# A graph layer's edge loop: where the softmax's exponentials, maxima and values stand in its steps

## The chip, the cores and the metric

The kernel runs on one core of one Trainium2 chip. The metric is the device time of one execution in microseconds. Before the change it is 4211.2 us, the median of three runs (4210.71 to 4215.71).

## The reference

12500 nodes with 128 features, 400000 edges in the order of their targets. Rows of node features are normalized and clipped, projected twice, gathered to the edges, weighted, and summed back to the targets with a softmax per target and head. Cut to what matters (`h` is the normalized input):

```python
message = (h @ w_src + b_src)[edge_src] + (h @ w_dst)[edge_dst]
rad_w = silu(silu(edge_attr_32 @ w1 + b1) @ w2 + b2) @ w3 + b3
message = (message * edge_weight1 * rad_w) @ w_sep + b_sep      # 8 heads of 16 + 16
alpha = smooth_leaky_relu(message[:, :, :16]); value = message[:, :, 16:]
score = einsum('ehk,ahk->eh', alpha, alpha_dot)
att = segment_softmax(score, edge_dst)                          # maximum, exp, sum per target
out = segment_sum(value * att, edge_dst) @ w_proj + b_proj
return x + out
```

`smooth_leaky_relu` contains a sigmoid, which the kernel computes through SiLU.

## The kernel before

A first stage normalizes the nodes and writes both projected tables (`t_src`, `t_dst`) to memory. The main loop, `step(k)` in `windows()`, then goes over the edges in NP = 391 pairs of sections; a section is SEC = 512 edges, a pair 1024. Its order is written out by hand: the functions are called in a fixed order in each step, and each engine runs its own instructions in that order. A step works on several pairs at once:

- `gather(k+2, f)` (L867): POOL issues 8 indirect transfers, one per 128 edges, into buffers of which there are three for each half `f`. `sources(k, f)` (L934) transposes the rows on PE into the banks `pm0` and `pm1`.
- The MLP on the edge attributes: `e_T(k+3)` (L877, L879), `mlp1(k+2)` (L886, two SiLUs at L890), `mlp2(k+1)` (L901, SiLU at L904), `mlp3(k)` (L918), `radial(k)` (L926).
- `split_md` (L852 to L859) cuts the targets' rows into three bf16 parts, on ACT and DVE in turn; `message(k)` (L941, L948) adds them and multiplies.
- `alphas(k-1, f)` (L954, SiLU at L956) and `alphas_sum` (L961); in odd steps `scores(k-2)` (L970, and `Sp` by an Identity on ACT, L987), whose result goes to memory, and once in MP = 8 steps comes back as `S_all` of a macro of 16 sections (L993).
- The softmax of macro m - 1 while macro m runs. With r = k modulo 8: `softmax_up` (L1003, L1008) at the end of r = 2, a scan for the running maximum; `softmax_down` (L1013), the scan back, and `softmax_exp` (L1018 subtraction, L1020 Exp, two stores of maxima at L1029) at the end of r = 3; `softmax_T` (L1035 transposes, L1038 copy) in two halves in r = 4.
- `weights(c)`, `values(c, f)`, `one_hot(c)` and `sums(c-1)` (L1045, L1065, L1067, L1051, L1078, L1082) with c = k - LAG, LAG = 13: values times weights, summed into windows of 64 targets by a product with a one-hot. The last loop steps, after k = NP, hold only this work (the tail). `store_win` and `store` (L1086, L1090) write the windows through SP. Stores to `agg` from step 384 on are declared free of the scatters (`2 * c + 1 >= (NC - 1) * (P // 2)`, NC = 13).

PSUM has few banks: the bank `misc` (`half` is its first half) serves the second half of `mlp1`, the window sums and the softmax's transposes in turn; the bank `m1` serves the first half of `mlp1`, the scores, the transposes of `e_T` and the spread of marks for the scans; `pa` and `V` have one buffer each.

Targets that cross a section's end are put together in blocks of 128 section ends: `block_load` and `block_rows`, `block_maxima`, `block_factors` (with two exponentials, L1158, L1159), `block_columns`, `block_totals`, `block_out`, run in the loop at fixed steps of each 32 (`stages`, from k = LATE + 32 j, LATE = 32 + LAG + 2) and for the last two blocks in the tail (`jobs`). In the tail the finished blocks are read back (`comb<-obs_d`) and scattered to `agg` by POOL (L1197). A last stage divides, projects and adds the input.

ACT computes SiLU and Exp with different function tables; a table is loaded (ACT_TABLE_LOAD) where the function changes.

Of the kernel before, what the change touches and what calls it, by code (L numbers as in the profile page):

```python
# [49 lines left out]
PR = 2 * SEC  # L50
MP = 8
MQ = 2 * MP
LAG = 13


@with_exitstack
def gnn_kernel(ctx: ExitStack, tc: tile.TileContext, a: dict, out: bass.AP):
# [694 lines left out]
    def windows():  # L752
# [7 lines left out]
        with tc.tile_pool(name="ps", bufs=1, space=PSUM) as pp, \  # L760
# [120 lines left out]
            def mlp1(k):  # L881

                p1 = [pp.tile([P, 2 * T], F32, name="m1"), half[:, 0:2 * T]]
                for q in range(2):
                    s = slice(q * 2 * RAD, (q + 1) * 2 * RAD)
                    nc.tensor.matmul(p1[q], w1b[s, :], eTs[k][s, :], start=True, stop=True)  # L886
                h1s[k] = sp.tile([P, SEC], F32, name="h1")
                h1v = h1s[k].rearrange("x (f p q) -> x q f p", f=2, q=2)
                for q in (1, 0):
                    nc.scalar.activation(h1v[:, q], p1[q].rearrange("x (f p) -> x f p", f=2),  # L890
                                         AF.Silu, bias=b12[:, 0:1], scale=1.0)
# [45 lines left out]
            def message(k):  # L937
                for j in range(3):
                    for f in range(2):
                        s, n = slice(f * W, (f + 1) * W), tiles(k, f) * T  # L940
                        nc.tensor.matmul(pms[k, f][:, 0:n], m3[k][s, j, :], ohT[k][s, 0:n],  # L941
                                         start=False, stop=(j == 2), skip_group_check=True)
                rad = rads.pop(k)
                mTs[k] = sp.tile([C, PR], F32, name="mT", bufs=LAG + 1)
                for f in range(2):
                    n = tiles(k, f) * T
                    s = slice(f * SEC, f * SEC + n)
                    nc.vector.scalar_tensor_tensor(mTs[k][:, s], pms.pop((k, f))[:, 0:n], b_n, rad[:, s],  # L948
                                                   op0=ALU.add, op1=ALU.mult)
# [64 lines left out]
                                             op0=ALU.add, op1=ALU.max)  # L1014

            def softmax_exp(m):
                M = Ms[m]
                nc.vector.tensor_sub(M[:, 0, :], S_all[m], M[:, 1, :])  # L1018
                Ps[m] = sp.tile([P, SEC], F32, name="Pr", bufs=1)
                nc.scalar.activation(Ps[m], M[:, 0, :], AF.Exp)  # L1020
                with nc.allow_non_contiguous_dma(reason="the maxima at the sections' ends"):
                    n = min(MQ, NS - m * MQ)
                    whole = MQ if n == MQ else n - 1
                    for e, q0, q1, o in ((0, 0, n, 0), (1, 0, whole, SEC - 1),
                                         (1, whole, n, E - 1 - (NS - 1) * SEC)):
                        if q1 > q0:
                            at = max_d[0:1, (m * MQ + q0) * 2 + e:(m * MQ + q0) * 2 + e + 1]
                            at = bass.AP(at.tensor, at.offset, [[2, q1 - q0], [2 * NS, H], [1, 1]])
                            nc.sync.dma_start(out=at, in_=M[q0 * H:q1 * H, 1, o:o + 1])  # L1029

            def softmax_T(m, i):
                pt = half[:T, :].rearrange("p (t q) -> p t q", t=TS // 2)
                t0 = i * (TS // 2)
                for t in range(TS // 2):
                    nc.tensor.transpose(pt[:, t, :], Ps[m][:, (t0 + t) * T:(t0 + t + 1) * T], ident)  # L1035
                if i == 0:
                    Pem[m] = sp.tile([T, TS, MQ, H], F32, name="Pem")
                nc.scalar.copy(Pem[m][:, t0:t0 + TS // 2].rearrange("p t q h -> p t (q h)"), pt)  # L1038
# [98 lines left out]

            def block_maxima(g):
                w, node = width(g), nodes.pop(g)
                differ[g] = sp.tile([P, P + 1], BF16, name="differ", bufs=1)  # L1140
                nc.vector.tensor_tensor(differ[g][:, 0:w], node[:, 1:w + 1], node[:, 0:w], op=ALU.not_equal)
                cuts[g] = sp.tile([P, P], BF16, name="cuts", bufs=1)
                nc.vector.tensor_scalar(cuts[g][:, 0:w], differ[g][:, 0:w], RESTART, None, op0=ALU.mult)
                ups[g] = sp.tile([P, P + 1], F32, name="up", bufs=2)
                if g:
                    nc.vector.tensor_copy(ups[g][:, 0:1], ups[g - 1][:, P:P + 1])
                else:
                    nc.vector.memset(ups[g][:, 0:1], 0.0)
                nc.vector.tensor_tensor_scan(ups[g][:, 1:1 + w], cuts[g][:, 0:w], mxs[g][:, 0:w],
                                             ups[g][:, 0:1] if g else RESTART, op0=ALU.add, op1=ALU.max)  # L1150

            def block_factors(g):
                w, up, mx = width(g), ups[g], mxs[g][:, 0:width(g)]
                de = des[g] = sp.tile([P, P], F32, name="de", bufs=2)[:, 0:w]
                nc.vector.tensor_add(de, up[:, 0:w], cuts.pop(g)[:, 0:w])
                nc.vector.tensor_sub(de, de, up[:, 1:1 + w])
                nc.vector.tensor_sub(mx, mx, up[:, 1:1 + w])
                nc.scalar.activation(de, de, AF.Exp)  # L1158
                nc.scalar.activation(mx, mx, AF.Exp)  # L1159
                nc.vector.tensor_mul(mx[:, 1:w:2], mx[:, 1:w:2], differ.pop(g)[:, 1:w:2])  # L1160

            def block_columns(g):
                w, rr = width(g), rrs.pop(g)
                rx = sp.tile([P, C], F32, name="rx", bufs=1)
                nc.scalar.copy(rx[:w].rearrange("p (h k) -> p h k", h=H),
                               rr[:w, C:ROW].unsqueeze(2).to_broadcast([w, H, C // H]))
                pt = small()
                nc.tensor.transpose(pt[:, 0, 0:w], rr[:w, 0:C], ident[:w, :w])
                nc.tensor.transpose(pt[:, 1, 0:w], rx[:w, :], ident[:w, :w])
                mx = mxs.pop(g)  # L1170
                tots[g] = [sp.tile([P, P], F32, name=n, bufs=2) for n in ("rn", "rd")]
                for k, r in enumerate(tots[g]):
                    nc.vector.tensor_mul(r[:, 0:w].rearrange("p (s i) -> p i s", i=2),
                                         pt[:, k, 0:w].rearrange("p (i s) -> p i s", i=2),
                                         mx[:, 0:w].rearrange("p (s i) -> p i s", i=2))
# [30 lines left out]
            def combined(g):  # L1206
# [1 line left out]
                return comb[g]  # L1208

            stages = {0: lambda g: (block_load(g), block_rows(g)), 2: block_maxima, 4: block_factors,  # L1210
                      5: block_columns, 6: block_totals, 8: block_out}
            assert LAST_M * MP == (NC - 1) * SB and NP - LAST_M * MP < MP and LATE + (NC - 3) * SB + 8 < NP


            def has(k):
                return 0 <= k < NP
# [4 lines left out]
            def step(k):  # L1221
# [54 lines left out]
                    split_md(k + 1, 2)  # L1276
                if has(k + 2):
                    mlp1(k + 2)
                if has(k):
                    mlp3(k)  # L1280
                if has(k + 1):
# [13 lines left out]
                if k == NP:  # L1295
                    alphas_sum(k - 1, 1, *alphas(k - 1, 1))
                    scores(k)
                if has(c):
                    values(c, 1)
                if has(k - MP) and r == 4:  # L1300
                    softmax_T(m - 1, 0)
                if has(k - 1) and k < NP:
                    sl = alphas(k - 1, 1)
                if has(k):
# [10 lines left out]
                    alphas_sum(k - 1, 1, *sl)  # L1315
                if has(k):
                    message(k)
                if has(k + 1):
                    mlp2(k + 1)
                if has(k - MP) and r == 4:  # L1320
                    softmax_T(m - 1, 1)
                if has(k - MP):
                    if r == 2:
                        softmax_up(m - 1)
                    elif r == 3:
                        softmax_down(m - 1)
                        softmax_exp(m - 1)
                j, o = divmod(k - LATE, SB)
                if 0 <= j < NC - 2 and o in stages:
                    stages[o](j)  # L1330

# [10 lines left out]
            def out_rows(g):  # L1342
# [4 lines left out]
                0: lambda: block_load(last - 1),  # L1347
                1: lambda: block_maxima(last - 1),
                2: lambda: block_factors(last - 1),
                5: lambda: block_load(last),  # L1350
                6: lambda: block_maxima(last),
                7: lambda: (block_factors(last), block_rows(last - 1)),
                8: lambda: block_columns(last - 1),
                9: lambda: block_totals(last - 1),
                10: lambda: out_rows(last - 1),
            }
            assert SB * (NC - 1) + LAG + 1 == NP + 7
            for k in range(NP, NP + LAG + 1):
                step(k)
                j = k - NP  # L1360
# [162 lines left out]
```

## Time and profile before

| what | value |
|---|---|
| median of three runs | 4211.2 us |
| the profiled execution | 4210.06 us, span of its instructions 4208.2 us |
| mean granted clock of TensorE | 0.978 |
| busy: PE, DVE, ACT, POOL | 93%, 74%, 45%, 72% of the span |
| gathers (L867) | 3125, 951 ns each |
| table loads on ACT | 49 to Exp at L1020, 48 back to SiLU at L956, 1283 ns each |
| PE's weight load at L1078 waiting for ACT's SiLU at L890 | 392.7 us in 371 waits |
| PE at L1078 waiting for the same | 108.2 us in 48 waits |

A row of a timeline has start, duration, engine, line, operation, output and inputs, count, and in brackets the idle time of the engine before it with what ended that. An instruction that only issues a transfer is shown with a q behind the engine's name. Loads of weights (PEld) overlap products (PE) and may wait long without PE standing.

### The profile page before, as it was taken

The numbers are of one execution on the slowest core, as the hardware profiler recorded it, in microseconds if no ns is written. First come the engines' busy times: TensorE is split into PE (matmuls) and PEld (weight loads), VectorE is DVE, ScalarE is ACT, GpSimd is POOL, SyncE is SP. The second block draws the span as 40 slices with busy tenths as digits, with TensorE's granted clock in tenths as the row PEclk, the third lists the DMA queues.
The fourth block names the chain that finished last, engine by engine and source line by source line (L and its number), as shares of the span: only waits on it lengthen the run. The fifth ranks groups of instructions, "written<-read, shape, count | busy, mean of one in ns | idle before, by whom it ended". The sixth has DMA issues, their size and how long they took to land. (4 is left out here: it accounts for less than half of the span.)

```text
span 4208.2 us, 87881 instructions
## 1 busy us (share of the span) xinstructions
PE 3917.1 (93%) x29351; PEld 2391.0 (57%) x29351; DVE 3103.4 (74%) x6187; ACT 1901.6 (45%) x4549; POOL 3009.4 (72%) x3195
## 2 busy tenths in 40 slices
PE   6789999999999999999999999999999999999975
PEld 6345555555555555555555555555555555555555
DVE  5567777777777777777777777777777777777754
ACT  5344444444444444444444444444444444444421
POOL 4767777777777777777777777777777777777710
PEclk8999999999999999999999999999999999999988
DMA  7766777777776776777777776776777676776624
GB/s 249 233 173 187 191 187 187 197 192 180 199 192 179 196 195 174 195 195 188 188 192 194 181 193 180 178 188 182 178 191 184 183 184 183 188 180 180 184 84 160
DMA packets 593334, 783.08 MB, mean 186 GB/s; under 512 B 125554, under 2 KB 392303, under 8 KB 592741
## 3 DMA queue, kind: packets, MB, share of 16 engines
q1 hardware_dynamic: 384786, 514.16, 40.9%
q0 software_dynamic: 100416, 205.44, 23.6%
q10 hardware_dynamic: 107666, 57.76, 4.6%
q8 instruction: 234, 3.83, 0.4%
q14 instruction: 232, 1.89, 0.2%
HBM read 637.83 MB, written 139.30 MB: 185 GB/s over the span
## 5 line engine op out<-in xcount | busy, mean ns | idle before, releaser
L867 POOL DMA_INDIRECT gs<-t_src,idx x3125 | 2971.5, 951 | 978.8 <-issue 801.7
L956 ACT ACTIVATE sl<-pa,c_b_a 128x512 f32<-128x512 f32 x782 | 536.9, 687 | 1021.1 <-PE pa L954 1009.5
L961 DVE SCALAR_TENSOR_TENSOR al<-pa,sl 128x512 f32<-128x512 f32 x782 | 539.8, 690 | 596.6 <-ACT sl L956 577.1
L1065 PEld LDWEIGHTS V<-c_w_v,mT 128*128 128x128 f32 x6048 | 746.7, 194 | 292.1 <-DVE ob L1082 119.1
L1065 PE MATMUL V<-c_w_v,mT 128*128 128x128 f32 x6048 | 879.3, 289 | 0.0
L954 PE MATMUL pa<-mT,c_w_a 128*128 128x512 f32 x1564 | 816.1, 604 | 4.0 <-DVE mT L948 3.0
L1067 DVE TENSOR_TENSOR pvx<-V,Pem 128x512 f32<-128x512 f32 x756 | 517.7, 685 | 243.8 <-PE V L1065 232.0
L934 PEld LDWEIGHTS pm<-ident,gs 128*128 128x128 f32 x3125 | 393.0, 142 | 422.1 <-issue 316.9
L1078 PEld LDWEIGHTS misc<-pvx,oh 128*64 128x64 f32 x6250 | 353.0, 137 | 407.8 <-ACT h L890 392.7
L926 DVE SCALAR_TENSOR_TENSOR rad<-p,c_fc_b,w_b 128x512 f32<-128x512 f32 x782 | 550.0, 745 | 40.1 <-PE p L918 3.5
L1078 PE MATMUL misc<-pvx,oh 128*64 128x136 f32 x6250 | 454.2, 287 | 115.4 <-ACT h L890 108.2
L948 DVE SCALAR_TENSOR_TENSOR mT<-pm,c_b_src,rad 128x512 f32<-128x512 f32 x782 | 550.6, 746 | 2.2 <-PE pm L941 2.2
L904 ACT ACTIVATE h<-p,b 128x512 f32<-128x512 f32 x391 | 287.6, 735 | 422.7 <-PE p L901 367.9
L934 PE MATMUL pm<-ident,gs 128*128 128x128 f32 x3125 | 471.0, 273 | 0.0
L918 PE MATMUL p<-h,w3b 64*128 64x512 f32 x1564 | 405.2, 595 | 14.4 <-ACT h L904 14.4
L941 PE MATMUL pm<-ohT,m 64*128 64x512 bf16 x2346 | 321.8, 380 | 0.0
L987 ACT ACTIVATE Sp<-m,b_s 128x512 f32<-128x512 f32 x192 | 131.9, 687 | 393.9 <-PE m L970 389.8
L886 PE MATMUL m<-eT,w1b 64*128 64x256 f32 x782 | 274.3, 431 | 17.9 <-DVE M L1008 16.7
L886 PE MATMUL misc<-eT,w1b 64*128 64x256 f32 x782 | 274.3, 431 | 0.0
L1051 DVE TENSOR_TENSOR oh<-lane,misc 128x504 f32<-128x504 f32 x391 | 261.3, 668 | 0.0
L901 PE MATMUL p<-h,w2b 64*64 64x256 f32 x3128 | 259.7, 402 | 1.0 <-DVE rad L926 1.0
L954 PEld LDWEIGHTS pa<-mT,c_w_a 128*128 128x128 f32 x1564 | 242.2, 196 | 20.0 <-DVE mT L948 7.1
(172 smaller groups left out, 3651.0 us busy)
## 6 DMA issues: line engine op xcount, KB each, us to landing
w_b<-in_edge_weight SPq DMA_DIRECT2D x390, 512.0 KB
d_b<-in_dst SPq DMA_DIRECT2D x390, 256.0 KB
gs<-t_src,idx POOLq DMA_INDIRECT x3125
e_t<-in_edge_attr ACTq DMA_DIRECT2D x390, 128.0 KB
sc_d<-Sp SPq DMA_DIRECT2D x192, 256.0 KB
win<-ob SPq DMA_DIRECT2D x391, 68.0 KB
agg<-ob SPq DMA_DIRECT2D x782, 33.5 KB
md<-t_dst SPq DMA_DIRECT2D x782, 32.0 KB
```

What stands on the lines that cost most here:

```text
L867: nc.gpsimd.indirect_dma_start(out=gs[:, t, :], out_offset=None, in_=t_src[:, :], in_offset=bass.IndirectOffsetOnAxis(ap=idx[:, t0 + t:t0 ...
L886: nc.tensor.matmul(p1[q], w1b[s, :], eTs[k][s, :], start=True, stop=True)
L918: nc.tensor.matmul(p3s[k][:, f, 0:SEC], w3b[s, :], h2s[k][s, :], start=True, stop=True)
L926: nc.vector.scalar_tensor_tensor(rad[:, s], p3[:, f, 0:n], b3, w_g[k][:, s], op0=ALU.add, op1=ALU.mult)
L934: nc.tensor.matmul(pms[k, f][:, t * T:(t + 1) * T], gs[:, t, :], ident, start=(t == 0), stop=False, is_transpose=True, skip_group_check=True)
L948: nc.vector.scalar_tensor_tensor(mTs[k][:, s], pms.pop((k, f))[:, 0:n], b_n, rad[:, s], op0=ALU.add, op1=ALU.mult)
L954: nc.tensor.matmul(pa[:, 0:n], w_a, mTs[k][:, f * SEC:f * SEC + n], start=True, stop=True)
L956: nc.scalar.activation(sl[:, 0:n], pa[:, 0:n], AF.Silu, bias=b_a, scale=1.0)
L961: nc.vector.scalar_tensor_tensor(al, pa, 0.25, sl, op0=ALU.mult, op1=ALU.add)
L1065: nc.tensor.matmul(V[:, t, :], mTs[c][:, o:o + T], w_v, start=True, stop=True)
L1067: nc.vector.tensor_mul(pvx[c][:, f, 0:n, 0:C].rearrange("p t (h k) -> p t h k", h=H), V[:, 0:n, :].rearrange("p t (h k) -> p t h k", h=H), ...
L1078: nc.tensor.matmul(acc[f * W:(f + 1) * W, :], ohs[c][:, f * TS + t, :], pvx[c][:, f, t, :], start=(t == 0), stop=(t == n - 1), skip_group_ ...
```

## The change

The exponential of the softmax leaves the end of step r = 3 and is issued in the middle of that step, after `mlp1` and before `mlp3`; the two exponentials of a block come right behind it, out of `block_factors`. So that its operand is there, both scans and the subtraction move to r = 2: the scan up before the second half of the values, the scan down and the subtraction (with the stores of the maxima) at the step's end. Both halves of the transposes move from r = 4 to r = 3, one after `message`, one at the step's end. The values then follow 12 steps behind (LAG = 12, one buffer of `mT` less). The blocks' stages start a step earlier, and from `block_columns` on stand where they stood; a multiplication moves from `block_factors` to `block_columns`, for which `differ` gets a second buffer. In the tail all jobs stand a step earlier, and there is one step less.

```diff
-LAG = 13
+LAG = 12
...
             def softmax_exp(m):
+                Ps[m] = sp.tile([P, SEC], F32, name="Pr", bufs=1)
+                nc.scalar.activation(Ps[m], Ms[m][:, 0, :], AF.Exp)
+
+            def softmax_sub(m):
                 M = Ms[m]
                 nc.vector.tensor_sub(M[:, 0, :], S_all[m], M[:, 1, :])
-                Ps[m] = sp.tile([P, SEC], F32, name="Pr", bufs=1)
-                nc.scalar.activation(Ps[m], M[:, 0, :], AF.Exp)
...
                 nc.vector.tensor_sub(mx, mx, up[:, 1:1 + w])
-                nc.scalar.activation(de, de, AF.Exp)
+
+            def block_exp(g):
+                nc.scalar.activation(des[g], des[g], AF.Exp)
+                mx = mxs[g][:, 0:width(g)]
                 nc.scalar.activation(mx, mx, AF.Exp)
-                nc.vector.tensor_mul(mx[:, 1:w:2], mx[:, 1:w:2], differ.pop(g)[:, 1:w:2])
...
-                      5: block_columns, 6: block_totals, 8: block_out}
+                      6: block_columns, 7: block_totals, 9: block_out}
...
                 if has(k + 2):
                     mlp1(k + 2)
+                j, o = divmod(k - LATE, SB)
+                if has(k - MP) and r == 3:
+                    softmax_exp(m - 1)
+                    if 0 <= j < NC - 2 and o == 5:
+                        block_exp(j)
                 if has(k):
                     mlp3(k)
...
+                if has(k - MP) and r == 2:
+                    softmax_up(m - 1)
                 if has(c):
                     values(c, 1)
-                if has(k - MP) and r == 4:
-                    softmax_T(m - 1, 0)
...
                 if has(k):
                     message(k)
+                if has(k - MP) and r == 3:
+                    softmax_T(m - 1, 0)
                 if has(k + 1):
                     mlp2(k + 1)
-                if has(k - MP) and r == 4:
-                    softmax_T(m - 1, 1)
                 if has(k - MP):
                     if r == 2:
-                        softmax_up(m - 1)
+                        softmax_down(m - 1)
+                        softmax_sub(m - 1)
                     elif r == 3:
-                        softmax_down(m - 1)
-                        softmax_exp(m - 1)
-                j, o = divmod(k - LATE, SB)
+                        softmax_T(m - 1, 1)
...
-                5: lambda: block_load(last),
-                6: lambda: block_maxima(last),
-                7: lambda: (block_factors(last), block_rows(last - 1)),
-                8: lambda: block_columns(last - 1),
-                9: lambda: block_totals(last - 1),
-                10: lambda: out_rows(last - 1),
+                3: lambda: block_exp(last - 1),
+                4: lambda: block_load(last),
+                5: lambda: block_maxima(last),
+                6: lambda: (block_factors(last), block_exp(last), block_rows(last - 1)),
+                7: lambda: block_columns(last - 1),
+                8: lambda: block_totals(last - 1),
+                9: lambda: out_rows(last - 1),
```

More of the change, by code (lines that the diff above doesn't have):

```diff
@@ L1139, in block_maxima @@
                 w, node = width(g), nodes.pop(g)
-                differ[g] = sp.tile([P, P + 1], BF16, name="differ", bufs=1)
+                differ[g] = sp.tile([P, P + 1], BF16, name="differ", bufs=2)
                 nc.vector.tensor_tensor(differ[g][:, 0:w], node[:, 1:w + 1], node[:, 0:w], op=ALU.not_equal)
@@ L1170, in block_columns @@
                 mx = mxs.pop(g)
+                nc.vector.tensor_mul(mx[:, 1:w:2], mx[:, 1:w:2], differ.pop(g)[:, 1:w:2])
                 tots[g] = [sp.tile([P, P], F32, name=n, bufs=2) for n in ("rn", "rd")]
@@ L1210, in windows @@
             stages = {0: lambda g: (block_load(g), block_rows(g)), 2: block_maxima, 4: block_factors,
-                      5: block_columns, 6: block_totals, 8: block_out}
-            assert LAST_M * MP == (NC - 1) * SB and NP - LAST_M * MP < MP and LATE + (NC - 3) * SB + 8 < NP
+                      6: block_columns, 7: block_totals, 9: block_out}
+            assert LAST_M * MP == (NC - 1) * SB and NP - LAST_M * MP < MP and LATE + (NC - 3) * SB + 9 < NP and (LATE + 5) % MP == 3
             def has(k):
@@ L1349, in windows @@
                 2: lambda: block_factors(last - 1),
-                5: lambda: block_load(last),
-                6: lambda: block_maxima(last),
-                7: lambda: (block_factors(last), block_rows(last - 1)),
-                8: lambda: block_columns(last - 1),
-                9: lambda: block_totals(last - 1),
-                10: lambda: out_rows(last - 1),
+                3: lambda: block_exp(last - 1),
[5 more added lines that the diff above has]
+                9: lambda: out_rows(last - 1),
             }
-            assert SB * (NC - 1) + LAG + 1 == NP + 7
+            assert SB * (NC - 1) + LAG + 1 == NP + 6
             for k in range(NP, NP + LAG + 1):
```

## The prediction

> **What bounds the kernel now.** I read the page first, then the gather's line in windows, then POOL's timeline against PE's. The page's line of engines, and one group of it:
>
> ```profile
> PE 3917.1 (93%) x29351; PEld 2391.0 (57%) x29351; DVE 3103.4 (74%) x6187; ACT 1901.6 (45%) x4549; POOL 3009.4 (72%) x3195
> ...
> L867 POOL DMA_INDIRECT gs<-t_src,idx x3125 | 2971.5, 951 | 978.8 <-issue 801.7
> ```
>
> PE looks like the bound, and POOL like an engine with a quarter of its time free. It isn't free: 801.7 of its 978.8 idle us are "issue", time in which it waited for nothing that the profile shows. POOL's timeline near the start of the loop and at its end, then two windows with the gather's line alone (length, busy us and count, clock, DMA share, GB/s):
>
> ```profile
> 240.73 0.94 POOL L867 DMA_INDIRECT gs<-t_src,idx  x1 [0.83 <-PE pm L934]
> ...
> 4008.24 0.95 POOL L867 DMA_INDIRECT gs<-t_src,idx  x1 [0.30 <-issue]
> 4009.50 0.94 POOL L867 DMA_INDIRECT gs<-t_src,idx  x1 [0.30 <-PE V L1065]
> ```
> ```profile
> 240.50:4010.50 3770.00, 2852.06 (x3001) 0.99 0.71 187
> 587.10:1339.60 752.50, 569.59 (x600) 1.00 0.73 191
> ```
>
> A gather takes 0.94 to 0.95 us, and 0.30 us pass before the next. The window from 587.10 begins and ends with a gather's start: 600 in 752.5 us, 1.254 us each. From the gather at 240.73 to the last are 3000 spacings in 3768.8 us, 1.256 each. So POOL runs at nearly its own best rate all through the loop. A period of 8 steps needs 64 gathers, 64 x 1.254 = 80.3 us, however fast the others are.
>
> PE over one such period: windows cut at the start of the MLP's third product (one per step); the first is a plain even step, then the steps with r = 2 and r = 4 (r is the step modulo 8), then the whole period. Columns: length; PE, PEld, DVE, ACT, POOL busy.
>
> ```profile
> 1962.11:1971.01 8.90, 8.90 (x70) 5.60 (x68) 7.14 (x15) 3.89 (x11) 6.74 (x8) 1.00 0.85 240
> 1980.91:1990.13 9.22, 9.22 (x71) 5.69 (x69) 8.10 (x16) 3.84 (x11) 6.78 (x9) 1.00 0.74 196
> 2000.42:2012.66 12.24, 9.58 (x74) 6.02 (x72) 7.50 (x17) 7.10 (x19) 9.23 (x10) 1.00 0.72 136
> 1962.11:2041.37 79.26, 76.60 (x586) 46.09 (x584) 60.79 (x120) 37.36 (x90) 60.04 (x64) 1.00 0.75 197
> ```
>
> PE is busy from end to end but for one step: at r = 4 it stands 12.24 - 9.58 = 2.66 us, and that is all that it stands in the period (79.26 - 76.60). The period takes 79.3 us, just under POOL's 80.3; one with a block's work is above it. The two engines run level. The last full group of gathers is issued by 4008.24 + 0.95 = 4009.19, and PE takes it up here:
>
> ```profile
> 4031.20 0.60 PE L934 MATMUL pm<-ident,gs 128*128 128x128 f32 x4
> ```
>
> 22.0 us later. That lead is what PE can gain on POOL, and nearly all of it.
>
> **Part 1, the exponential leaves the end of the step.** The chain from r = 3 into 4, ACT's timeline, then PE's:
>
> ```profile
> 1998.01 1.28 ACT L1020 ACT_TABLE_LOAD   x1
> 1999.92 0.63 ACT L1020 ACTIVATE Pr<-M 128x512 f32<-128x512 f32 x1 [0.63 <-DVE M L1018]
> 2000.46 0.28 ACT L852 CAST m<-md 128x128 bf16<-128x128 f32 x1
> ...
> 2000.99 1.28 ACT L956 ACT_TABLE_LOAD   x1
> 2002.29 0.69 ACT L956 ACTIVATE sl<-pa,c_b_a 128x512 f32<-128x512 f32 x1
> ```
> ```profile
> 2003.61 0.34 PE L1078 MATMUL misc<-pvx,oh 128*64 128x136 f32 x2 [2.17 <-ACT h L890]
> ```
>
> Load, a wait of 0.63 us for the subtraction, Exp, and the load back push the next step's SiLUs back, and the window sums, whose bank they read, stand 2.17 us. The whole stall of the step is the 2.66 us above, and I take it to go. Changed, two loads and Exp, 1.28 + 0.63 + 1.28 = 3.2 us, lie between the first layer's SiLUs and the second alpha's SiLU of r = 3. ACT's idle gaps there now:
>
> ```profile
> 1993.30 0.69 ACT L987 ACTIVATE Sp<-m,b_s 128x512 f32<-128x512 f32 x1 [2.06 <-PE m L970]
> 1995.28 0.69 ACT L956 ACTIVATE sl<-pa,c_b_a 128x512 f32<-128x512 f32 x1 [1.29 <-PE pa L954]
> ```
>
> 2.06 + 1.29 = 3.35: it fits. A load is not held by its operand's wait (it ended at 1999.29, and Exp waited on), and the cast right behind Exp shows that a copy needs no load; Sp, an Identity, I take to be of that kind. Queued behind Exp are Sp, the second SiLU, the copy of eT with the issue of the next e_t load, the copy of Pem and the second layer's SiLU: some tenths late each. PE waits for Sp before the transposes of e_t, which share its bank. Taken 0; bounds 0 and 1.0 us a period, the upper one for the periods, one in four, in which a block's two exponentials come behind it.
>
> The Trainium skill, ScalarE: Activation LUTs, section What ACT_TABLE_LOAD costs, gives about 1283 ns for a load, as in the trace, and a drain of about 1380 ns beside it, which no row here shows: the SiLU starts 0.02 us after its load. By the page's 2.66 us a switch, an estimate, the move would be 2.6 us too long for its gaps and cost up to that.
>
> **Part 2, the maxima a step sooner.** Both scans and the subtraction now stand in r = 2 on DVE. Its timeline there, and the two operations that r = 3 has now:
>
> ```profile
> 1984.18 0.68 DVE L1067 TENSOR_TENSOR pvx<-V,Pem 128x512 f32<-128x512 f32 x1
> 1984.78 0.28 DVE L859 TENSOR_TENSOR m<-mr,m 128x128 bf16<-128x128 f32 x1
> 1985.78 0.69 DVE L961 SCALAR_TENSOR_TENSOR al<-pa,sl 128x512 f32<-128x512 f32 x1 [0.72 <-ACT sl L956]
> 1986.40 1.41 DVE L948 SCALAR_TENSOR_TENSOR mT<-pm,c_b_src,rad 128x512 f32<-128x512 f32 x2
> 1987.73 1.21 DVE L1008 TENSOR_TENSOR_SCAN M<-m,S 128x512 f32<-128x512 f32 x1
> ```
> ```profile
> 1997.95 1.21 DVE L1013 TENSOR_TENSOR_SCAN M<-m,M 128x512 f32<-128x512 f32 x1
> 1999.20 0.69 DVE L1018 TENSOR_TENSOR M<-S,M 128x512 f32<-128x512 f32 x1
> ```
>
> DVE is busy 7.14 of a plain even step's 8.90 us; 1.21 + 1.21 + 0.69 = 3.11 more make 10.25, in a step of 9.54 (two spreads of marks on PE at 0.32, from 9.22 - 8.90). DVE runs over by 0.7. Behind the late subtraction stand the product with V, the rest of md, its cast on ACT, the SiLUs behind that, and PE's window sums of r = 3. I count 0.5 us of PE there (a tenth or two of slack); bounds 0 and 1.9, the two operations that come new. The transposes go to r = 3 at their old cost. The stores of the maxima on SP wait for the same scan a step earlier; the stores and the loads behind them wait as they did. POOL's gathers are moved past nothing.
>
> PE's period is then 79.26 - 2.66 + 0.5 = 77.1 us against POOL's 80.3. PE uses up the lead in some ten periods, and from there on waits for gathers.
>
> **Part 3, the start.** The scan waited once for the scores' way through memory, and then POOL for PE:
>
> ```profile
> 222.70 1.22 DVE L1008 TENSOR_TENSOR_SCAN M<-m,S 128x512 f32<-128x512 f32 x1 [16.37 <-DMA S<-sc_d]
> ```
> ```profile
> 229.87 0.94 POOL L867 DMA_INDIRECT gs<-t_src,idx  x1 [9.15 <-PE m L877]
> ```
>
> The landing stays where it is (SP's queue ahead of it is the same), but the scan now stands ahead of half a step of DVE's work: 0.28, 0.69, 1.41, then the scan down and the subtraction, 1.21 + 0.69, before the next step goes on. POOL's wait grows by these 4.3 us (bounds 0 and 8).
>
> **Part 4, values 12 steps behind.** A step's products move from the tail into the loop, where POOL hides them, and the tail has a step less. Its steps are spaced so (SP, then POOL):
>
> ```profile
> 4080.70 1.81 SPq L1090 DMA_DIRECT2D agg<-ob  x2
> 4082.62 0.36 SPq L1364 DMA_DIRECT2D comb<-obs_d  x1
> ...
> 4087.37 1.83 SPq L1090 DMA_DIRECT2D agg<-ob  x2
> ```
> ```profile
> 4085.17 0.97 POOL L1197 DMA_INDIRECT agg<-comb,ids  x1 [5.69 <-DMA comb<-obs_d]
> ```
>
> A store to agg of a step below 384 waits for the scatter before it. The tail's first such step is 380 before and 381 after, so this chain has three links, not four: -6.7 us (bounds -3 and -10).
>
> **The sum,** against the profiled execution's 4210.06 us. The lead of 22.0 us shrinks to the time a gather takes to land. I take 2.5 us for it, an estimate from the transfer above (issued at 4082.62, awaited until 4085.17): -19.5. POOL's stream at 1.254 all through: 3000 x 1.2542 - 3768.8 = -6.2. Start +4.3, tail -6.7. Together -28.1: 4182.0. The median, 4211.2, is 1.1 above the profiled time: 4183. About 0.2%, 8 us, is what a measurement of this kernel can tell from no change.
>
> **Rivals.**
> (a) POOL can go faster, its 0.30 us being slack that PE's pace asks for. Then 2.66 - 0.5 us come in each of 48 periods: 4211.2 - 104 + 4.3 - 6.7, about 4105. For it speaks PE's 93%. Against it, the spacing of 1.254 holds in windows where POOL waits for no one. Chance 0.06. Perfetto Trace Analysis in the Trainium skill, section Identifying the Most-Contended Engine, measures GpSimd by occupancy; by that rule POOL at 72% bounds nothing, and this rival would be the forecast.
> (b) The stall only moves. DVE's overfull r = 2 and ACT's tight r = 3 cost the 2.7 us again; start and tail alone are left, 4211.2 + 4.3 - 6.7, so 4200 to 4212 with their bounds. For it: the upper bounds of parts 1 and 2 add to 2.9. Against: PE's waits there begin only where gaps of 3.35 are overfilled. Chance 0.17.
> (c) Slower: the first scan, in the middle of the step, comes before its scores have landed. Their load is issued here, and the scan would take the place of pvx at 1984.18, 6.5 us later, where it had 10.05:
>
> ```profile
> 1977.68 0.56 SPq L993 DMA_DIRECT2D S<-sc_d  x1
> ```
>
> The scan's row at 1987.73 shows no wait, so landing takes at most 10.05; DVE, and PE behind it, would stand up to 3.5 us in each period. That is 48 x (3.5 + 0.5 - 2.7) = +62 at most, with start and tail +60, 4271; it decides from landings at about 9 us. For it: DMA engines busy 0.71 of the time, and the wait of 16.37. Against: that wait was the only one. Chance 0.09.
>
> **How the numbers follow.** The forecast has 0.68. Its bounds (start 0 to 8, tail -10 to -3, POOL's spacing 1.2475 to 1.256, between 0.94 + 0.30 and the mean now) give 4160 to 4193. The range goes on to 4202, which takes in a third of (b). Left out are (a), (c) and the last of (b), 0.2 with the forecast's own edges. Faster by over 0.2%: the forecast, (a) and half of (b), 0.82; the same: the rest of (b), 0.09; slower: (c), 0.09.
>
> **What would show it.** Right: POOL's gathers at 1.254 without a wait for PE; in late periods PE waiting for gathers in front of its transposes; no wait for h of 2 us at r = 4; the last full group taken up within 3 us; a tail one step shorter. Wrong: gathers closer than 1.24 us (a); waits of PE at r = 2 and 3 that add to 2.7 us (b); the first scan waiting for S in every period (c).

## The result, and the profile after

The changed kernel takes 4189.8 us (median of 5 runs, 4182.5 to 4197.9), the kernel before 4211.2 (5 runs, 4210.0 to 4215.7): a ratio of 0.9948, 95% interval 0.9936 to 0.9960. The forecast was 4183, with a range of 4160 to 4202. The profiled execution took 4188.98 us, its span 4187.2, 21.0 less than the span before.

First the page's line of engines after the change and the gather's group, then the gather's line alone in 3000 us of the loop (length, POOL's busy us and count, clock, DMA share, GB/s):

```profile
PE 3920.8 (94%) x29351; PEld 2372.0 (57%) x29351; DVE 3092.3 (74%) x6187; ACT 1897.7 (45%) x4549; POOL 3008.3 (72%) x3195
...
L867 POOL DMA_INDIRECT gs<-t_src,idx x3125 | 2970.4, 951 | 980.7 <-issue 783.4
```
```profile
600.00:3600.00 3000.00, 2271.46 (x2391) 1.00 0.73 188
```

From the first gather in this window to the last it is 1.255 us each, against 1.256 in the same window of the kernel before. POOL's stream hardly changed. What changed is who waits at its other end. PE's waits, and POOL's longest ones (us in total, times, longest):

```profile
PE pm L934 <- DMA gs<-t_src,idx: 76.3, 95, 2.5
...
PE misc L1080 <- ACT h L890: 12.8, 19, 1.1
PE misc L1037 <- ACT Pem L1040: 9.2, 26, 0.8
```
```profile
POOL gs L867 <- issue: 783.4, 2569, 0.6
POOL gs L867 <- PE pm L934: 54.9, 136, 13.8
```

PE's 108.2 us of waits for the SiLU at the window sums are down to 12.8. In their place it waits 76.3 us, in 95 waits, for gathers in front of their transposes. These rows date the stream's pieces, from POOL's first gather to the last full group and to PE's taking it up (POOL, then PE), and then SP's reading back of `agg` at the tail's end; the rows of before that the prediction does not show follow:

```profile
75.57 1.18 POOL L867 DMA_INDIRECT gs<-t_src,idx  x1 [14.23 <-DMA t_dst<-ms]
...
231.01 0.94 POOL L867 DMA_INDIRECT gs<-t_src,idx  x1 [13.79 <-PE pm L934]
...
246.31 0.94 POOL L867 DMA_INDIRECT gs<-t_src,idx  x1 [0.30 <-issue]
...
4010.17 0.94 POOL L867 DMA_INDIRECT gs<-t_src,idx  x1 [0.30 <-issue]
```
```profile
4014.64 0.60 PE L934 MATMUL pm<-ident,gs 128*128 128x128 f32 x4
```
```profile
4116.24 3.83 SPq L1411 DMA_DIRECT2D g<-agg  x7
```
```profile
73.65 1.18 POOL L867 DMA_INDIRECT gs<-t_src,idx  x1 [13.53 <-DMA t_dst<-ms]
```
```profile
4137.46 2.58 SPq L1401 DMA_DIRECT2D g<-agg  x5
```

The gather at 246.31 is the one that stood at 240.73 before. Piece by piece, where the 21.0 us came from:

| piece | before | after | change |
|---|---|---|---|
| start to the first gather | 73.65 | 75.57 | +1.9 |
| from there to the gather at 240.73 (246.31) | 167.08 | 170.74 | +3.7 |
| from there to the issue of the last full group | 3768.46 | 3764.80 | -3.7 |
| from there until PE takes it up (the lead) | 22.01 | 3.53 | -18.5 |
| from there to the reading back of `agg` | 106.26 | 101.60 | -4.7 |
| rest | 70.74 | 70.96 | +0.2 |

The lead is nearly the whole gain. Step by step through the loop, PE's lead on the gathers shrinks over the first nine periods of the softmax; from there on its smallest value in a period lies between 2.2 and 4.3 us, but for two periods with some 6. The -3.7 of the stream is not shown to come from the change: in two variants of the changed kernel that leave POOL's order alone (below, LAG = 13 and the scan moved back) the same stretch takes 3766.9 and 3768.7 us.

### The profile page after: what moved, and what is told of

Read it like the earlier page. It is cut to its first block, busy times and chain, and to the rows that moved or that the text cites. A ratio compares the mean times of both kernels' runs of the same rounds, so it can differ in the third digit from the quotient of the medians.

```text
span 4187.2 us, 87937 instructions
## 1 busy us (share of the span) xinstructions
PE 3920.8 (94%) x29351; PEld 2372.0 (57%) x29351; DVE 3092.3 (74%) x6187; ACT 1897.7 (45%) x4549; POOL 3008.3 (72%) x3195
## 5 line engine op out<-in xcount | busy, mean ns | idle before, releaser
L1067 PEld LDWEIGHTS V<-c_w_v,mT 128*128 128x128 f32 x6064 | 737.5, 192 | 298.4 <-DVE ob L1084 153.4
L1067 PE MATMUL V<-c_w_v,mT 128*128 128x128 f32 x6064 | 867.6, 286 | 0.0
L954 PE MATMUL pa<-mT,c_w_a 128*128 128x512 f32 x1564 | 805.7, 597 | 3.6 <-DVE mT L948 2.7
L934 PE MATMUL pm<-ident,gs 128*128 128x128 f32 x3125 | 498.1, 276 | 78.4 <-DMA gs<-t_src,idx 76.3
L1080 PE MATMUL misc<-pvx,oh 128*64 128x136 f32 x6250 | 453.5, 287 | 18.0 <-ACT h L890 12.8
L918 PE MATMUL p<-h,w3b 64*128 64x512 f32 x1564 | 405.9, 596 | 13.5 <-ACT h L904 13.4
L890 ACT ACTIVATE h<-misc,b 128x256 f32<-128x256 f32 x391 | 193.0, 494 | 150.1 <-PE misc L886 148.7
```

Of the source, the lines that this page charges most:

```text
L918: nc.tensor.matmul(p3s[k][:, f, 0:SEC], w3b[s, :], h2s[k][s, :], start=True, stop=True)
L934: nc.tensor.matmul(pms[k, f][:, t * T:(t + 1) * T], gs[:, t, :], ident, start=(t == 0), stop=False, is_transpose=True, skip_group_check=True)
L954: nc.tensor.matmul(pa[:, 0:n], w_a, mTs[k][:, f * SEC:f * SEC + n], start=True, stop=True)
L1067: nc.tensor.matmul(V[:, t, :], mTs[c][:, o:o + T], w_v, start=True, stop=True)
L1080: nc.tensor.matmul(acc[f * W:(f + 1) * W, :], ohs[c][:, f * TS + t, :], pvx[c][:, f, t, :], start=(t == 0), stop=(t == n - 1), skip_group_ ...
```

## Experiments

**Is POOL the bound, and how much does PE gain?** Two kernels make POOL cheaper: the eighth gather of each step is left out, in the kernel before and in the changed one.

```diff
-                for t in range(tiles(k, f)):
+                for t in range(min(tiles(k, f), TS - f)):
...
-                    nc.tensor.matmul(pms[k, f][:, t * T:(t + 1) * T], gs[:, t, :], ident,
+                    nc.tensor.matmul(pms[k, f][:, t * T:(t + 1) * T], gs[:, min(t, TS - f - 1), :], ident,
```

The kernel before, cut:

> The kernel before with 7 gathers per step in place of 8 (the last tile's rows of each pair are not gathered; the tile before it is taken twice), so that POOL needs 56 x 1.254 = 70.2 us for a period of 8 steps. Theory (before, PE was at its own pace and POOL just level): PE's period stays at 80.3 us on average, time within 15 us of 4211, 4196 to 4212, and POOL now waits for PE's buffers. Rival (POOL already held PE back before): time falls by over 40 us.

The changed kernel, cut:

> The changed kernel with the same 7 gathers per step. Theory (the change frees some 2.5 us of PE in each period, and POOL's 80.3 us hide it): with POOL at 70.2 us the period falls to PE's own, about 77.8 us as in the periods before the lead was used up, so 4085 to 4115 us, and POOL waits for PE. Rival (the stall only moved to the steps with r = 2 and 3, and POOL is not what holds): 4175 to 4190, as with 8 gathers.

Measured: 4206.6 us for the first (ratio 0.9986 to the kernel before, 0.9977 to 0.9996) and 4094.7 for the second (0.9722, 0.9707 to 0.9737). Both came as the theory said. In the kernel before, an eighth off POOL's work brings 4.6 us, since PE's pace lies just above; POOL then waits for PE, as its waits in the cut kernel show:

```profile
POOL gs L867 <- PE m L877: 466.9, 373, 16.7
```

In the changed kernel the same cut brings 95 us. So the change is worth 111.9 us where PE sets the pace (the mean period of steps 40 to 383 falls from 80.31 to 78.10 us, which makes 106 in 48 periods), and 21.4 with all gathers: POOL hides 90. The same block-free period as in the prediction, in the cut kernel before and in the cut changed one (length; PE, PEld, DVE, ACT, POOL busy):

```profile
1957.87:2037.13 79.26, 76.60 (x585) 46.12 (x583) 61.01 (x120) 37.33 (x90) 52.90 (x57) 1.00 0.73 190
```
```profile
1911.13:1988.03 76.90, 76.60 (x585) 46.06 (x583) 60.76 (x120) 37.00 (x90) 53.11 (x57) 1.00 0.76 196
```

PE's work is 76.60 us in both. Standing time falls from 2.66 to 0.30 us a period.

**What do the steps behind bring?** The changed kernel with LAG = 13 again (`mT` keeps the changed kernel's 13 buffers, which the kernel sets in a line not shown here; the blocks' stages stay where the change put them, the tail's last jobs stand a step later):

> The changed kernel with the values 13 steps behind again (LAG = 13, the blocks' stages at the same steps as in the changed kernel, the tail's jobs of the last block a step later, as before the change). Theory (the tail's removed step was worth what its chain of stores and scatters costs): 5 to 7 us slower than the changed kernel, about 4195; the gathers and the lead as in the changed kernel. Rival (the tail's length is set by the softmax of the last macro and the last block, not by the count of steps): no difference, 4186 to 4192.

```diff
-LAG = 12
+LAG = 13
...
-            LATE = SB + LAG + 2
+            LATE = SB + 14
```

Measured: 4195.4 us (ratio 0.9961, 0.9947 to 0.9974), 5.6 above the changed kernel; the profiled executions are 9.0 apart. Most of that is the tail: from PE's taking up the last group to the reading back of `agg` it is 4125.84 - 4017.44 = 108.4 us here, 101.6 in the changed kernel, 106.3 in the one before. A step less is worth 6.8 us there, and nothing shows that it is worth anything in the loop.

```profile
4017.44 0.60 PE L934 MATMUL pm<-ident,gs 128*128 128x128 f32 x4
```
```profile
4125.84 6.70 SPq L1411 DMA_DIRECT2D g<-agg  x10
```

The chain that the prediction counts shows as well, in SP's waits for a scatter ahead of a store to `agg` (us in total, times, longest): four in the kernel before, three in the changed one, four with LAG = 13.

```profile
SPq L1090 <- DMA agg<-comb,ids: 21.3, 4, 11.9
```
```profile
SPq L1092 <- DMA agg<-comb,ids: 10.6, 3, 4.4
```
```profile
SPq L1092 <- DMA agg<-comb,ids: 16.7, 4, 7.2
```

**What does the scan in the middle of the step cost at the start?** The changed kernel with the first macro's scan up moved back to the end of its step:

> The changed kernel, with the first macro's scan up alone at the end of step r = 2 (all later ones in the middle). Theory (half a step of DVE's work stands behind the wait for the first scores): POOL's wait there falls from 13.8 to about 9 us, and the time by 3 to 5 us, to about 4185. Rival (the wait's length is set by the landing alone, or the gain is lost again before the lead is used up): wait and time as in the changed kernel, 4188 to 4191.

```diff
-                if has(k - MP) and r == 2:
+                if has(k - MP) and r == 2 and m > 1:
                     softmax_up(m - 1)
...
+                        if m == 1:
+                            softmax_up(m - 1)
                         softmax_down(m - 1)
```

Measured: 4186.7 us (ratio 0.9944, 0.9930 to 0.9957). POOL's longest wait for PE is 10.7 us, 3.1 less than in the changed kernel where some 4.8 were expected, and the median is 3.1 lower. But the two intervals overlap, so it is not shown that this kernel is faster. The profiled executions, 3.0 us apart, don't show it either: from the first gather to the one at 246.31 (here at 241.79) 2.7 us are gained, and the stream behind takes 3.9 more; the difference stands ahead of the first gather (1.8), in the lead (1.3) and behind the reading back of `agg` (1.9), less 0.8 in the tail. That the gain at the start is lost again, as the rival has it, stays possible.

```profile
POOL gs L867 <- PE pm L934: 52.4, 138, 10.7
```

**Does the load back to SiLU cost anything?** In the changed kernel's trace the load back waits for the product of the step. ACT at r = 3:

```profile
1979.33 1.28 ACT L1018 ACT_TABLE_LOAD   x1
1980.62 0.63 ACT L1018 ACTIVATE Pr<-M 128x512 f32<-128x512 f32 x1
1981.20 0.69 ACT L987 ACTIVATE Sp<-m,b_s 128x512 f32<-128x512 f32 x1
1983.16 1.28 ACT L956 ACT_TABLE_LOAD   x1 [1.27 <-PE pa L954]
...
1984.46 0.69 ACT L956 ACTIVATE sl<-pa,c_b_a 128x512 f32<-128x512 f32 x1
```

The first load starts at once behind the SiLUs. The second stands idle 1.27 us until `pa` is there, and only then loads for 1.28. In ACT's order the SiLU's wait for PE is an instruction of its own, and it stands ahead of the load. A kernel takes that wait off the load, in the cut form, where PE is the bound: a SiLU of one element a row directly behind the exponentials.

> The changed kernel with the eighth gather of each step left out (the tile before it is used twice) and one SiLU of one element a row directly behind the exponentials, with no operand of the step's: the load back to SiLU then stands ahead of that one and waits for nothing of PE. Theory (the load back takes over the wait for pa of the first SiLU, so that it starts only when pa is there, and what stands behind it on ACT, h of the first window and the copy of Pem, is late by a load): the waits for Pem and h shorten and the time falls from 4094.7 us to 4075 to 4090 us. Rival (the load would have been done in ACT's gap anyway, or another engine sets the step): 4092 to 4100 us.

```diff
+            def silu_back():
+                one = sp.tile([P, 1], F32, name="one", bufs=1)
+                nc.scalar.activation(one, eps, AF.Silu)
...
                     softmax_exp(m - 1)
                     if 0 <= j < NC - 2 and o == 5:
                         block_exp(j)
+                    if has(k):
+                        silu_back()
```

Measured: 4094.5 us (ratio 0.9723, 0.9707 to 0.9739), against 4094.7. ACT at r = 3 shows that the load goes off right behind Exp:

```profile
1944.41 0.63 ACT L1018 ACTIVATE Pr<-M 128x512 f32<-128x512 f32 x1
1945.04 1.28 ACT L1022 ACT_TABLE_LOAD   x1
1946.34 0.20 ACT L1022 ACTIVATE one<-eps 128x1 f32<-128x1 f32 x1
1946.45 0.67 ACT L987 ACTIVATE Sp<-m,b_s 128x512 f32<-128x512 f32 x1
```

PE's wait for the copy of `Pem` at r = 3, 14.3 us in 42 periods in the cut changed kernel, is gone. But Sp and the SiLUs behind it come later by the load, and PE now waits for those: 2.9 us for Sp, in the eleven periods with a block, and at r = 5 some 1.5 more for each of the two layers' SiLUs. The period's mean falls by 0.15 us, from 78.10 to 77.95, and the time stays. The theory's range is missed and the rival's met: the wait is there, and it costs nothing that the times show. They would not show the 7 us that 0.15 us in 48 periods make, as each interval is 6 us to either side.

**Are the loads the cause of the old stall?** The kernel before, cut, with SiLU in the place of Exp, so that nothing is loaded in the loop:

> The kernel before with 7 gathers per step, and SiLU in place of all exponentials of the loop, so that ACT loads no table there (the results are not the softmax's). Theory (the two loads in the chain from r = 3 to r = 4 make the stall that the change removes): the wait of 2.2 us for h at r = 4 falls below 0.3 us, and the time from 4206.6 to 4085 to 4110 us, where the changed kernel with 7 gathers is. Rival (the subtraction and Exp at the end of the step make the stall, the loads are hidden): 4190 to 4206.

```diff
-                nc.scalar.activation(Ps[m], M[:, 0, :], AF.Exp)
+                nc.scalar.activation(Ps[m], M[:, 0, :], AF.Silu)
...
-                nc.scalar.activation(de, de, AF.Exp)
-                nc.scalar.activation(mx, mx, AF.Exp)
+                nc.scalar.activation(de, de, AF.Silu)
+                nc.scalar.activation(mx, mx, AF.Silu)
```

Three more runs of this kernel:

> The kernel before with the eighth gather of each step left out (the tile before it is used twice), and with SiLU in the place of the exponential in the loop, so that ACT's function is loaded once and not twice a period; the probabilities are no longer probabilities, the number and shapes of all instructions stay. Theory (the 2.66 us that PE stands at r=4 come from the two loads of ACT's function around the exponentials): PE's period falls as in the changed kernel with the same cut (4094.7 us), 4085 to 4110 us. Rival (they come from the exponentials' own time or from DVE's queue): 4190 to 4206 us, as the kernel before with the cut (4206.6 us).

> The kernel before with the eighth gather of each step left out (the tile before it is used twice), and with SiLU in the place of the exponential in the loop, so that ACT's function is loaded once and not twice a period; the probabilities are no longer probabilities, the number and shapes of all instructions stay. Theory (the 2.66 us that PE stands at r=4 come from the two loads of ACT's function around the exponentials): PE's period falls as in the changed kernel with the same cut (4094.7 us), 4085 to 4110 us. Rival (they come from the exponentials' own time or from DVE's queue): 4190 to 4206 us, as the kernel before with the cut (4206.6 us).

> The kernel before with the eighth gather of each step left out (the tile before it is used twice), and with SiLU in the place of the exponential in the loop, so that ACT's function is loaded once and not twice a period; the probabilities are no longer probabilities, the number and shapes of all instructions stay. Theory (the 2.66 us that PE stands at r=4 come from the two loads of ACT's function around the exponentials): PE's period falls as in the changed kernel with the same cut (4094.7 us), 4085 to 4110 us. Rival (they come from the exponentials' own time or from DVE's queue): 4190 to 4206 us, as the kernel before with the cut (4206.6 us).

Two further runs of the cut changed kernel with `silu_back`:

> The changed kernel with 7 gathers per step and, right behind the exponentials, a SiLU of one element per partition that waits for nothing, so that the load back to SiLU stands there and not behind the wait for pa. Theory (in the changed kernel the load back carries the wait of the SiLU behind it, starts only when pa is done, and so makes that SiLU, the copy of eT and the first copy of Pem late): the second half of the softmax's transposes no longer waits 0.3 us for the copy, 5 to 20 us faster than 4094.7, so 4075 to 4090. Rival (the lateness is hidden, PE waits for something else there): 4092 to 4100.

> The changed kernel with the eighth gather of each step left out (the tile before it is used twice) and one SiLU of one element a row directly behind the exponentials, with no operand of the step's: the load back to SiLU then stands ahead of that one and waits for nothing of PE. Theory (the load back takes over the wait for pa of the first SiLU, so that it starts only when pa is there, and what stands behind it on ACT, h of the first window and the copy of Pem, is late by a load): the waits for Pem and h shorten and the time falls from 4094.7 us to 4075 to 4090 us. Rival (the load would have been done in ACT's gap anyway, or another engine sets the step): 4092 to 4100 us.

All four, the two further runs of the cut changed kernel with `silu_back` and the run of the next experiment were on chips on which the kernel before itself takes 5309 to 5355 us. Medians: 4792.8, 4788.6, 4792.9 and 4725.1 us here (ratios 0.8889 to 0.8965 to the kernel before there), and 4688.3 and 4690.0 for the cut changed one with `silu_back` (0.8764 and 0.8752). The theory would have the two alike, and the first stays some 100 us above (35 in the last run, on a chip that is itself faster; some 75 there by the ratios). It would fail by that, if these chips showed the kernel's ordinary waits; the last section tells why they don't. On them the step of r = 4 is still 3.1 to 3.7 us longer than its neighbours without any load, but most of that is a wait for DVE's one-hot (longest of PE's waits in the second run):

```profile
PE misc L1035 <- DVE oh L1054: 114.6, 47, 3.2
```

In the kernel before on an ordinary chip that wait is 20.2 us in 34, and the wait for `h` 108.2 in 48. On the chips of these four runs the wait for `h` at r = 4 is shorter without being gone: 28 to 34 us in 21 to 24 of 43 steps. So the runs leave open whether the two loads, Exp itself or DVE's queue make the old stall. The rows of the kernel before set a limit, though. The load to Exp ended at 1999.29, 0.63 us before the subtraction let Exp start, and so was not in the chain. Only the load back was, 1.28 us of the 2.17; without it some 0.9 us would be left for Exp and the late subtraction, an estimate from these rows. By that estimate the theory, which has both loads make the stall, would fail on an ordinary chip too.

**Can the start be relieved otherwise?** The changed kernel with the zeroing of `agg` issued three steps earlier:

> The changed kernel with the stores that clear agg issued three steps earlier on SP (from step -3, not from 0). Theory (POOL's one long wait, 13.8 us near step 14, comes from the first macro's scores standing on SP and in the DMA queues behind those stores): that wait falls by 8 us or more, and as POOL is the bound, the time by as much, to 4172 to 4183. Rival (the clearing stores only delay other loads then, or the first scan waits as long): 4186 to 4195.

```diff
-                if 0 <= 2 * k < NZ:
-                    for i in range(2 * k, min(2 * k + 2, NZ)):
+                if 0 <= 2 * (k + 3) < NZ:
+                    for i in range(2 * (k + 3), min(2 * (k + 3) + 2, NZ)):
```

5233.5 us on such a chip (ratio 0.9777, 0.9749 to 0.9804). The changed kernel was not run there, so the time is inconclusive. The trace speaks for the theory: the first scan waits for nothing, and POOL's longest wait near step 14 is 2.9 us, where two runs of the cut changed kernel with `silu_back` on such chips have 9.5 and 7.3 us for the scan and 10.3 and 9.2 for POOL. As those kernels differ in more than the zeroing, it isn't shown.

## Why the prediction was right

**The bound.** Right. POOL's spacing held at 1.255 us, and the cut kernels show it from the other side. Rival (a), POOL faster when PE asks for it, is out: PE waits 76.3 us for gathers, and POOL still keeps 0.30 us between them. What (a) would have been worth is measured, though: 4094.7 us once POOL is cheap, near the prediction's 4105. On the occupancy rule of Perfetto Trace Analysis in the Trainium skill, section Identifying the Most-Contended Engine, the runs decide against it here: POOL stays at 72% and bounds the changed kernel, where an eighth of its gathers is worth 95 us.

**Part 1.** The stall went; PE's wait for `h` fell as forecast. One sub-step failed: "A load is not held by its operand's wait". It holds for Exp's load and not for the load back, which waited for `pa` in 45 periods, 53.2 us in all. The price of 0 was nearly right all the same: the load's lateness costs PE the wait for the copy of `Pem` (part 2), and taking it away with the one-element SiLU brought 0.15 us a period. The reading of the old chain was off too, as the first load was not in it (above). The drain of about 1380 ns that the Trainium skill gives (ScalarE: Activation LUTs, section What ACT_TABLE_LOAD costs) again shows in no row: Exp starts 0.01 us behind its load and the SiLU 0.02 us behind the other.

**Part 2.** The 0.5 us of standing in r = 3 was right in the mean and not in its place. A block-free period keeps 0.30 us, of which 0.28 is the wait for the copy of `Pem`, so it takes 76.9 and not 77.1; that wait comes from part 1's load back. PE's window sums, which the prediction has late in every period, wait in r = 3 only in the eleven periods with a block, 9.6 us in all. There `block_factors` now stands at the end of r = 2, and its three operations on DVE (0.29, 0.29 and 0.28 us) come on top of the overrun. So in the cut changed kernel (DVE, then PE):

```profile
2170.38 0.69 DVE L1022 TENSOR_TENSOR M<-S,M 128x512 f32<-128x512 f32 x1
2170.98 0.29 DVE L1157 TENSOR_TENSOR de<-up,cuts 128x128 f32<-128x128 f32 x1
```
```profile
2173.38 1.15 PE L1080 MATMUL misc<-pvx,oh 128*64 128x136 f32 x16 [0.82 <-ACT h L890]
```

The two kinds of wait make 0.56 us a period in the mean, 0.22 of it by what the prediction names. The overfull r = 2 takes 9.6 us, as forecast (9.54). In the mean of all periods, blocks included, the cut pair's steps change by +0.4 us at r = 2, +0.9 at r = 3 and -3.7 at r = 4, the period from 80.31 to 78.10; work that moved is in these (a spread of marks of 0.32 us from r = 3 to r = 2, the transposes, 0.68 us, from r = 4 to r = 3). Rival (b), the stall moving as a whole, is out by that. Rival (c) too: of the loop's scans up only the first waits for its scores, and in the tail that of the last macro,

```profile
DVE M L1008 <- DMA S<-sc_d: 19.1, 1, 19.1
...
DVE M L1008 <- DMA S<-Sp: 1.9, 1, 1.9
```

so that the others found theirs landed.

**Parts 3 and 4, and the sum.** Term by term, forecast against measured: the lead -19.5 against -18.5 (the pick-up follows 3.5 us behind the issue, not 2.5, nor within the 3 that the prediction names as a sign); POOL's stream -6.2 against -3.7; the start +4.3 against +5.6; the tail -6.7 against -4.7; the rest 0.2. The differences add up to 7.0 us, all in one direction, and that is the distance of 4182.0 from 4188.98. The 2.5 us were taken from a plain load. Where PE stood for a gather, in the changed kernel, it used it a median of 5.7 us behind the end of its issue (3.2 to 7.8). That the lead came out near is partly luck: PE takes up a group at the first of its four gathers, issued some 3.8 us (three spacings) before the last. Of the start's +5.6, 3.7 go with the scan, near the forecast, POOL's wait growing from 9.15 to 13.79; 2.7 of them are gone where the scan is moved back. 1.9 lie ahead of the first gather, where the code is the same, and are a difference between executions: the other runs on such chips have that gather at 73.3 to 74.3. The worst-sized term is POOL's stream. The prediction gave it one window's 1.2542 all through; the mean went from 1.2563 to 1.2550 only, which the variants' scatter covers. The lead was used up in nine periods, as forecast (some ten). In the tail the step less was sized right: against LAG = 13 it saves 6.8 us. What the term left out is that with LAG = 13 the changed kernel's tail is 2.1 us longer than before the change, 108.4 against 106.3. 1.8 of it lie behind the end of the last window sums (12.9 us to the reading back before, 14.7 with LAG = 13, 16.1 in the changed kernel); what makes it so is open. In the range two sums don't come out: all bounds at once give 4155 to 4196 and not 4160 to 4193, and the chances left out are 0.06, 0.09 and two thirds of 0.17, that is 0.26 and not 0.2.

## What to carry to other kernels

An engine at 72% can be the bound: look at the spacing of its own instructions against the work of a period, not at its share. Where two engines run level, what is taken from one is worth only its lead over the other, here 18.5 of some 106 us, and the lead can be read before the change as the time from the last issue to its use, less what a transfer needs to land. To learn what a change frees behind another bound, make the other engine cheaper in both kernels and compare those two.

## What the runs showed of the hardware

**A stand of PE can halve the clock behind it.** In the kernel before, 16 of the 43 steps with r = 4 between steps 40 and 383 hold a stretch of 3.41 us in which TensorE's granted clock is 0.5, beginning within 1.6 us of the end of a stand of PE; none of the other steps there holds one. A block-free step with one takes 13.1 to 13.4 us, one without 12.2 to 12.4. In windows, one such step (length; PE, PEld, DVE, ACT, POOL busy; clock):

```profile
2079.69:2092.93 13.24, 11.01 (x76) 7.07 (x74) 7.67 (x17) 7.09 (x19) 9.89 (x12) 0.87 0.72 149
```

All these stretches begin on one grid of 3.41 us, and the grid parts the two cases. Of the block-free steps' stands, 2.2 us long, all 13 that began up to 0.4 us ahead of a grid line or up to 0.8 behind one were followed by such a stretch, and none of the 19 that began 1.6 to 3.0 us behind one. In the changed kernel the loop has three such stretches, in its variants with the scan moved back and with LAG = 13 six and eight. So the old stall cost 2.66 us and in two of five periods 0.9 more. A period at clock 1.00, as the prediction takes it, does not hold that. The mean granted clock went from 0.978 to 0.984.

**On some chips DVE starts late behind PE's products.** On the chips with 5309 to 5355 us, DVE's product with `V`, where it had to wait for PE, began a median of 1.6 to 2.0 us behind the recorded end of PE's product; on the others 0.04 us. ACT's results reach DVE 0.03 us behind on both. One such pair, PE's last product of the group ending at 2394.18 and DVE's start:

```profile
2393.02 1.16 PE L1071 MATMUL V<-c_w_v,mT 128*128 128x128 f32 x8
```
```profile
2396.40 0.69 DVE L1073 TENSOR_TENSOR pvx<-V,Pem 128x512 f32<-128x512 f32 x1 [2.65 <-PE m L877]
```

What makes it so was not found. Matmul ends are modelled in the trace, so that PE itself may be the slower one.
